# Group norms, key centring and scaled weights with PSUM operands or on ScalarE; joins that carry the ends of child stages

## The chip, the cores and the metric

The kernel runs on one core of one Trainium2 chip. The metric is the device time of one execution in microseconds, as a median of several runs. A profile is one more execution, taken by the hardware profiler. Its engines are PE (TensorE), PEld (TensorE's weight loads), DVE (VectorE), ACT (ScalarE), POOL (GpSimd) and SP (SyncE, which here only issues DMAs).

## The reference, cut to what matters

The input is x, eight images of 56 x 56 x 192 in float32. Two layers follow each other, each of them a group norm, a block and a residual.

```python
def _gn(v, G=32, eps=1e-5):          # 32 groups of 6 channels, over all positions
    g = v.reshape(B, H, W, G, C // G)
    m = mean(g, axis=(1, 2, 4)); s = var(g, axis=(1, 2, 4))
    return ((g - m) / sqrt(s + eps)).reshape(v.shape)

# layer 0: attention with convolved projections
q  = pointwise(batch_norm(depthwise3x3(_gn(x), stride 1)))   # 3136 tokens, 3 heads of 64
kv = pointwise(batch_norm(depthwise3x3(_gn(x), stride 2)))   # 784 keys
x  = x + softmax(q k^T * 64**-0.5) v @ out_w + out_b

# layer 1: a selective scan in four directions
xa, z = split(in_proj_w @ _gn(x))              # 384 channels each
xc = silu(depthwise3x3(xa) + conv_b)
for k in range(4):                             # row-wise, column-wise, and both reversed
    dts, Bs, Cs = split(x_proj_weight[k] @ xc)
    delta = softplus(dt_projs_weight[k] @ dts + dt_projs_bias[k])
    h = exp(delta * A) * h + delta * B * xc    # 16 states per channel, along 3136 positions
    y += sum_over_states(h * C) + D * xc
x = x + (layernorm(y) * silu(z)) @ out_proj_w.T
```

## The kernel before, in words

An image is worked in seven chunks of T = 448 positions (NCH = 7), with the channels on the partitions: 192 channels are two blocks (NB) of 96 (CP), 384 are three (NJ) of 128.

**The scan** is the long part. For each image there are four directions (in the order 0, 1, 3, 2), seven chunks and 16 states, thus 448 steps. A step takes these turns: `inputs_made` has POOL form du times the broadcast row of B into one of seven h buffers (L1175); `decays` has ACT form exp(delta * A) into a PSUM bank (L1189); `scans` has DVE run the recurrence, three instructions for the three blocks (L1206), and `carries` keeps its last column (L1228). Of 16 states, POOL scales and adds three by C itself (L1304, L1308); for the others PE transposes h (L1252, four bundles of three), ACT scales the result by C (L1268) and PE transposes back into the accumulator y (L1286). DVE adds y into yacc at a chunk's end (L1338, L1340). The rows of B and C come by DMA as broadcasts (`bb`, five buffers, and `cb`).

**The preparation** of the next image runs beside the scan of this one. `front` loads the image, transposes it and takes its statistics (`part`), forms the group norm's scale and shift (`group_norm`), normalizes (`normal`, ACT, L538), convolves and projects to q, k and v, centres the keys and bounds the scores (the loop over `kts`, L693 to L707), attends, takes the second group norm, scales the input weights by it (`scaled_weights`, L475), projects and convolves. `x_proj` then makes the scan's inputs; its last stores are `du<-v`. `finish` normalizes yacc, gates it and projects it out; it scales the z weights anew, as `wz2`, once per image.

**The group norm** (`group_norm`, L447 to L465) merges the chunks' statistics per channel on DVE (bn_aggr), averages mean and variance over each group of six channels by a matmul with the block matrix `group`, squares the distance of the channel's mean from the group's, averages that by a second matmul, and forms rstd by Ln and Exp on ACT.

**The keys**: for each of three heads, DVE sums the keys over their 784 positions (L693), divides (L694), subtracts the mean from `kT` (L696), takes the largest absolute value (L698) and multiplies it into the bounds of q (`km`, L700). PE adds over the partitions (L703), and DVE turns the sums into the shift of the exponents, `nsh` (L706, L707).

**The order of the work** is written by a list scheduler that runs when the program is built (`Sched`). A stage is a generator that yields requests: engine, estimated cost, the cells it reads and writes. A cell holds the estimated time of its last write and read; a DMA's write comes at its stated latency plus MARGIN, 3.0 us. The scheduler gives out the request with the earliest t - rank, where t is not before the stage's start nor the engine's estimated free time. The result is a fixed order of instructions on each engine, and each engine works through its own in that order; semaphores alone hold it up. `front` is paced by the scan's progress (`pace`): within 12 us of PE time of a wanted share. PE gets small filler matmuls (L1418) where the plan leaves it a gap.

A stage's `start` bounds all its requests, and a child inherits it. `join` waits until the children are done and lifts the parent's `start` to their `end`. A stage's own `end` grows with its own requests alone. `arounds` runs, for each image, the stages `front(b + 1)` and then `x_proj(b + 1)`, each by a join; both do most of their work in children of their own.

SBUF for the preparation comes from pools that are opened and closed in turn, so that a tile of one stage can lie where a tile of the stage before it lay; the instruction that first writes it waits for the last reader. The two `pad` tiles of `front`, whose border columns are set to zero by four memsets (L511), are the first tiles written in an image's preparation.

Of the kernel before, what the change touches and what calls it, by code (L numbers as in the profile page):

```python
# [8 lines left out]
F32 = mybir.dt.float32  # L9
AF = mybir.ActivationFunctionType  # L10
ALU = mybir.AluOpType
# [8 lines left out]
CP = 96  # L20
NB = C // CP
# [6 lines left out]
HEADS, DH = 3, 64  # L28
KW = HW // 2
KEYS = KW * KW  # L30
# [4 lines left out]
NJ = DIN // 128  # L35
# [19 lines left out]
PE, ACT, DVE, POOL, SP = range(5)  # L55
# [110 lines left out]
class Sched:  # L166
# [25 lines left out]
    def join(self, stages):  # L192

        me = self.now
        yield lambda: all(s.done for s in stages)
        me.start = max([me.start] + [s.end for s in stages])

    def keep_busy(self, t):

# [75 lines left out]
def kernel(  # L275
# [24 lines left out]
    nc = tc.nc  # L300
# [21 lines left out]
    group = fill("group", [CP, CP], 1.0 / 6.0)  # L322
# [31 lines left out]
    for nm, src in (("q", bn_q), ("kv", bn_kv)):  # L354
        p = load(f"bn{nm}", [CP, 4, NB], src.rearrange("v (b p) -> p v b", p=CP))
        s = const.tile([CP, NB], F32, name=f"bns{nm}")
# [66 lines left out]
    gnp = ctx.enter_context(tc.tile_pool(name="gn", bufs=2))  # L423
# [10 lines left out]
    def bank():  # L434
        return banks[0]

    def group_norm(st, cells, layer):

        mv = gnp.tile([CP, NB, 2], F32, name="mv")
        gm = gnp.tile([CP, NB, 2], F32, name="gm")  # L440
        mean = gnp.tile([CP, NB], F32, name=f"mean{layer}")
        dm = gnp.tile([CP, NB], F32, name="dm")
        rstd = gnp.tile([CP, NB], F32, name=f"rstd{layer}")
        k = [Cell() for _ in range(6)]
        yield DVE, 0.3, cells, [k[0]]
        for bl in range(NB):
            nc.vector.bn_aggr(mv[:, bl, :], st[:, bl])  # L447
        pg = yield bank()
        yield PE, 0.2, [k[0]], pg.c
        nc.tensor.matmul(pg.ap[:CP, 0:2 * NB], group, mv.rearrange("p b s -> p (b s)"), start=True, stop=True)  # L450
        yield DVE, 0.6, pg.c, [k[1]]
        nc.vector.tensor_copy(gm.rearrange("p b s -> p (b s)"), pg.ap[:CP, 0:2 * NB])
        pg.free()
        nc.vector.tensor_copy(mean, gm[:, :, 0])
        nc.vector.tensor_tensor(dm, mv[:, :, 0], mean, ALU.subtract)
        nc.vector.tensor_tensor(dm, dm, dm, ALU.mult)
        pd = yield bank()
        yield PE, 0.2, [k[1]], pd.c
        nc.tensor.matmul(pd.ap[:CP, 0:NB], group, dm, start=True, stop=True)
        yield DVE, 0.2, pd.c, [k[2]]  # L460
        nc.vector.tensor_tensor(rstd, pd.ap[:CP, 0:NB], gm[:, :, 1], ALU.add)
        pd.free()
        yield ACT, 0.5, [k[2]], [k[3]]
        nc.scalar.activation(rstd, rstd, AF.Ln, bias=eps[:CP])
        nc.scalar.activation(rstd, rstd, AF.Exp, scale=-0.5)  # L465
        return mean, rstd, k[3]

    def scaled_weights(w, cell, half, rstd, k):

        got = Cell()  # L470
        yield SP, 0.07, [], [got], 5.0
        nc.sync.dma_start(w, in_wT.rearrange("(b p) o -> p b o", p=CP)[:, :, half * DIN:(half + 1) * DIN])
        yield DVE, 0.6, [got, k], [cell]
        for bl in range(NB):
            nc.vector.tensor_scalar(w[:, bl], w[:, bl], rstd[:, bl:bl + 1], None, ALU.mult)  # L475

    def dma(reads, writes, late, dst, src, after=()):
        yield SP, 0.07, reads, writes, late
# [7 lines left out]
    def front(b):  # L486
# [12 lines left out]
        st = gnp.tile([CP, NB, NCH, 6], F32, name="st")  # L499
        with tc.tile_pool(name=f"fx_{b}", bufs=2) as pool:  # L500
            fx = Rings(pool, 2)
            k_st = [Cell() for _ in range(NCH)]
# [39 lines left out]
                               pad.ap, [pad])  # L542

            yield from sc.join([sc.spawn(part(c)) for c in range(NCH)])
            mean, rstd, k_rs = yield from group_norm(st, k_st, 0)
            off, k_gn = gnp.tile([CP, NB], F32, name="off"), Cell()
            yield DVE, 0.3, [k_rs], [k_gn]
            nc.vector.scalar_tensor_tensor(off, mean, -1.0, rstd, ALU.mult, ALU.mult)
            yield from sc.join([sc.spawn(normal(c)) for c in range(NCH)])

        with tc.tile_pool(name=f"kv_{b}", bufs=1) as kvp:
# [7 lines left out]
            k_qm = [[Cell() for _ in range(NCH)] for _ in range(2)]  # L559
# [8 lines left out]
            qms = [kvp.tile([128, NCH], F32, name=f"qm{i}") for i in range(2)]  # L568
# [117 lines left out]
            pn = yield bank()  # L686
            for h, kt in enumerate(kts):
                kk = [Cell() for _ in range(4)]
                ks = gnp.tile([128, 1], F32, name=f"ks{h}")
                kx = gnp.tile([128, 1], F32, name=f"kx{h}")  # L690
                km = kvp.tile([128, NCH], F32, name=f"km{h}")
                yield DVE, 1.1, k_k[h // 2] + [k_z], [kk[0]]
                nc.vector.tensor_reduce(ks, kt, AX.X, ALU.add)  # L693
                nc.vector.tensor_scalar(ks, ks, 1.0 / KEYS, None, ALU.mult)  # L694
                yield DVE, 0.6, [kk[0]], [kk[1]]
                nc.vector.tensor_scalar(kt, kt, ks, None, ALU.subtract)  # L696
                yield DVE, 0.9, [kk[1]], [kk[2]]
                nc.vector.tensor_reduce(kx, kt, AX.X, ALU.max, apply_absolute_value=True)  # L698
                yield DVE, 0.1, [kk[2]] + k_qm[h // 2], [kk[3]]
                nc.vector.tensor_scalar(km, qms[h // 2], kx, None, ALU.mult)  # L700
                k_km.append(kk[1])
                yield PE, 0.1, [kk[3]], pn.c if h == HEADS - 1 else []
                nc.tensor.matmul(pn.ap[:TP, h * NCH:(h + 1) * NCH], ones, km, start=True, stop=True)  # L703
            nv = nsh.rearrange("p h c -> p (h c)")
            yield DVE, 0.3, pn.c, [k_ns]
# [4 lines left out]
            st1 = gnp.tile([CP, NB, NCH, 6], F32, name="st1")  # L710
            k_st1 = [Cell() for _ in range(NCH)]
# [90 lines left out]
                yield from sc.join(ends)  # L802


        mean1, rstd1, k_gn1 = yield from group_norm(st1, k_st1, 1)
        nbias = gnp.tile([128, 2 * NJ], F32, name="nbias")
        k_nb = Cell()
        with tc.tile_pool(name=f"fw_{b}", bufs=1) as fw, tc.tile_pool(name=f"fi_{b}", bufs=2) as pool:
# [6 lines left out]
            pn = yield bank()  # L815
            for i, w in enumerate((wx, wz)):
                yield PE, 1.2, [k_w[i], k_gn1], pn.c if i else []
                for j in range(NJ):
                    for bl in range(NB):
                        nc.tensor.matmul(pn.ap[:, i * NJ + j:i * NJ + j + 1], w[:, bl, j * 128:(j + 1) * 128],  # L820
                                         mean1[:, bl:bl + 1], start=(bl == 0), stop=(bl == NB - 1))
            yield DVE, 0.1, pn.c, [k_nb]
            nc.vector.tensor_scalar(nbias, pn.ap[:, :2 * NJ], -1.0, None, ALU.mult)
            pn.free()
            made[b] = dict(
                x1d=x1d, xcs=xcs, k_x1=k_x1, k_xcs=k_xcs, rstd=rstd1, nbias=nbias, k_gn=k_gn1, k_nb=k_nb,
# [295 lines left out]
    chunks, brow, crow, das, states, news, ys = {}, {}, {}, {}, {}, {}, {}  # L1122
# [107 lines left out]

    def y_of(i):

        if i not in ys:
            t = yield ry
            free = Cell()
            free.w = t.c[0].r
            at["y"] = i
            ys[i] = dict(t=t, free=free, on=False, left=[(NST - len(by[i])) * SUB + sum(z for _, z in by[i].values())] * NJ)
        return ys[i]
# [105 lines left out]
    with tc.manual_schedule():  # L1345
# [11 lines left out]
        with ExitStack() as es:  # L1357
# [4 lines left out]
            ry = Ring(lambda: ybanks, 1)  # L1362
# [127 lines left out]
```

## Time and profile before

| | |
|---|---|
| median of 3 runs | 17656.52 us (17656.25 to 17665.69) |
| profiled execution | 17659.74 us, span 17658.0 us |
| granted TensorE clock, mean | 0.973 |
| PE, PEld, DVE, ACT, POOL busy | 15853.6, 11086.3, 14092.1, 14192.0, 15553.4 us |
| DMA moved, mean rate | 2373.32 MB, 134 GB/s |

The busy times are averages over stages with different limits, so they are read together with stretches of the span. A group of instructions is told by its line, engine, operation, output and inputs; the mean duration is that of one instruction and includes any time for which it is held up once it has been issued. Idle time before an instruction is put down to what ended it.

### The profile page before, as it was taken

The page shows a single profiled execution, that of the slowest core. Times are in us where ns is not written, and L with a number is a line of the kernel's source. Part 1 is how long each engine was busy: PE and PEld are TensorE (multiplying, and loading weights), DVE is VectorE, ACT ScalarE, POOL GpSimd, SP SyncE. Part 2 cuts the span into 40 slices and gives each one's busy share as a digit, 9 for nine tenths or more (in the row PEclk, how much of TensorE's full clock was granted, in tenths as well). Part 3 has the DMA queues.
Part 4 walks back from the last instruction along what each step waited for, and adds up shares of the span by engine and source line. Part 5 has one row for each costly group of instructions (what it writes and reads, how often), then busy time and mean ns, then how long its engine had stood idle before and what let it go on. Part 6 is the DMA issues. An engine that isn't in the chain of part 4 may idle for free. (4 is left out here: it accounts for less than half of the span.)

```text
span 17658.0 us, 282202 instructions
## 1 busy us (share of the span) xinstructions
PE 15853.6 (90%) x101550; PEld 11086.3 (63%) x101550; DVE 14092.1 (80%) x17871; ACT 14192.0 (80%) x25030; POOL 15553.4 (88%) x5200
## 2 busy tenths in 40 slices
PE   7699989998989989899898998989989898999998
PEld 4366666666666656666566666666656666667776
DVE  2378877888778878788787887878878888789898
ACT  3478887788877888788787887878888788889888
POOL 0489889898998989899898998989989899899998
PEclk9899999999999999999999999999999999999999
DMA  2653465435553365533645336453364434643332
GB/s 75 203 163 98 131 180 154 115 98 158 157 162 110 99 165 160 158 101 100 177 154 155 100 99 188 146 154 98 104 194 145 143 101 116 181 146 115 96 101 77
DMA packets 1508343, 2373.32 MB, mean 134 GB/s; under 512 B 197104, under 2 KB 1498912, under 8 KB 1503872
## 3 DMA queue, kind: packets, MB, share of 16 engines
q1 hardware_dynamic: 1506944, 2355.25, 45.8%
q8 instruction: 806, 13.21, 0.3%
q14 instruction: 593, 4.86, 0.1%
HBM read 1803.75 MB, written 550.97 MB: 133 GB/s over the span
## 5 line engine op out<-in xcount | busy, mean ns | idle before, releaser
L1206 DVE TENSOR_TENSOR_SCAN h<-da,newc,h 128x448 f32<-128x448 f32 x9216 | 10083.4, 1136 | 1717.6 <-ACT da L1189 1400.8
L1175 POOL TENSOR_TENSOR h<-du_s,bb 128x1344 f32<-128x1344 f32 x3584 | 10827.0, 3055 | 598.0 <-PE ht L1252 506.4
L1189 ACT ACTIVATE da<-dl_s,acoef 128x448 f32<-128x448 f32 x10752 | 6589.3, 636 | 839.2 <-DVE h L1206 420.2
L1268 ACT ACTIVATE g<-ht,ct_s 112x384 f32<-112x384 f32 x10864 | 5943.0, 578 | 1330.8 <-PE ht L1252 1123.0
L1252 PE MATMUL ht<-ident,h 128*112 128x128 f32 x32592 | 5209.4, 278 | 317.7 <-DVE h L1206 225.3
L1286 PE MATMUL y<-ident,g 112*128 112x112 f32 x32592 | 4909.1, 269 | 619.0 <-ACT g L1268 479.3
L1286 PEld LDWEIGHTS y<-ident,g 112*128 112x128 f32 x32592 | 3532.2, 142 | 2599.9 <-ACT g L1268 1663.8
L1252 PEld LDWEIGHTS ht<-ident,h 128*112 128x112 f32 x32592 | 3677.1, 135 | 1012.9 <-DVE h L1206 458.4
L1206 DVE TENSOR_TENSOR_SCAN h<-da,h 128x448 f32<-128x448 f32 x1536 | 1589.9, 1076 | 331.6 <-ACT da L1189 240.7
L1304 POOL TENSOR_TENSOR h<-h,cb 128x1344 f32<-128x1344 f32 x420 | 1282.0, 3052 | 476.4 <-DVE newc L1228 245.2
L1418 PE MATMUL y<-zeros 128*128 128x64 f32 x12318 | 1650.9, 272 | 0.0
L1418 PEld LDWEIGHTS y<-zeros 128*128 128x128 f32 x12318 | 1591.7, 197 | 56.7 <-issue 56.6
L1304 POOL TENSOR_TENSOR yp<-h,cb 128x1344 f32<-128x1344 f32 x448 | 1367.0, 3051 | 274.7 <-DVE h L1206 165.7
L1308 POOL TENSOR_TENSOR yp<-yp,h 128x1344 f32<-128x1344 f32 x420 | 1279.4, 3046 | 32.8
L1323 PE MATMUL y<-yp,ident 128*128 128x448 f32 x2688 | 1221.3, 552 | 7.4 <-POOL yp L1308 7.0
L976 POOL TENSOR_TENSOR v<-v,xs 128x1344 f32<-128x1344 f32 x224 | 678.6, 3050 | 591.3 <-DMA dl<-v 586.1
L782 PE MATMUL bank<-qT,kT 128*112 128x448 f32 x2352 | 1054.1, 566 | 141.0 <-DVE oT L745 90.1
L791 PE MATMUL bank<-pT,vt 112*128 112x448 f32 x2352 | 1019.1, 544 | 25.8 <-ACT pT L732 21.5
L732 ACT ACTIVATE pT<-bank,nsh 112x448 f32<-112x448 f32 x1176 | 743.6, 634 | 198.4 <-PE bank L782 159.5
L782 PEld LDWEIGHTS bank<-qT,kT 128*112 128x112 f32 x2352 | 360.6, 177 | 534.6 <-DVE oT L745 120.0
L1009 PE MATMUL bank<-xd,dtw 128*128 128x448 f32 x1344 | 632.9, 572 | 39.9 <-DVE h L1206 10.5
L1228 DVE TENSOR_REDUCE newc<-h 128x3 f32<-128x3 f32 x3584 | 563.2, 157 | 103.7
(146 smaller groups left out, 9950.6 us busy)
## 6 DMA issues: line engine op xcount, KB each, us to landing
bb<-rows SPq DMA_DIRECT2D x3584, 224.0 KB, 3.4
cb<-rows SPq DMA_DIRECT2D x868, 224.0 KB, 3.6
dl<-v SPq DMA_DIRECT2D x224, 672.0 KB, 5.1
du<-v SPq DMA_DIRECT2D x224, 672.0 KB, 5.2
du_s<-du SPq DMA_DIRECT2D x224, 672.0 KB, 4.5
dl_s<-dl SPq DMA_DIRECT2D x224, 672.0 KB, 4.5
stack<-xpd SPq DMA_DIRECT2D x504, 232.0 KB, 5.0
xt<-x1d SPq DMA_DIRECT2D x224, 336.0 KB, 5.7
```

Source lines behind the costliest of these rows:

```text
L782: nc.tensor.matmul(ps.ap[:TP, :T], kts[h][:, kb * TP:(kb + 1) * TP], qh.ap, start=True, stop=True)
L791: nc.tensor.matmul(po.ap[:, :T], vt[:, kb, g:g + 2, :].rearrange("p g d -> p (g d)"), pts[kb].ap, start=(kb == 0), stop=(kb == NKB - 1))
L1175: nc.gpsimd.tensor_tensor(h.ap, du.ap, bb.ap.unsqueeze(1).to_broadcast([128, NJ, T]), ALU.mult)
L1189: nc.scalar.activation(da.ap[:, :T], dl.ap[:, j], AF.Exp, scale=acoef[:, k * NJ + j, n:n + 1])
L1206: nc.vector.tensor_tensor_scan(h.ap[:, j, rev], da.ap[:, 0:T][:, rev], h.ap[:, j, rev], news[i - 1].ap[:, j, n:n + 1] if ci else 0.0, ALU. ...
L1252: nc.tensor.transpose(ht.ap[:TP, j * 128:(j + 1) * 128], h.ap[:, j, s * TP:(s + 1) * TP], ident)
L1268: nc.scalar.activation(g.ap, ht.ap[:TP, :DIN], AF.Copy, scale=ct.ap[:, s, n:n + 1])
L1286: nc.tensor.matmul(y["t"].ap[:, j, s * TP:(s + 1) * TP], g.ap[:, j * 128:(j + 1) * 128], ident[:TP, :TP], is_transpose=True, start=(n == 0 ...
L1304: nc.gpsimd.tensor_tensor(to.ap, h.ap, cbr.ap.unsqueeze(1).to_broadcast([128, NJ, T]), ALU.mult)
L1308: nc.gpsimd.tensor_tensor(yp.ap, yp.ap, h.ap, ALU.add)
L1323: nc.tensor.matmul(y["t"].ap[:, j, :T], ident, yp.ap[:, j], start=False, stop=(y["left"][j] == 0))
L1418: nc.tensor.matmul(ybanks[:, 0, T:T + FILL], zeros, zeros[:, :FILL], start=False, stop=False)
```

## The change

In `Sched.join` the parent's `end` is lifted to its new `start`, so that a stage whose work lies in children hands their end on to the stage that joins it.

`group_norm` copies the group's values out of PSUM no longer before it uses them. The differences take the group's mean from PSUM, one of the two factors of the square is itself written to PSUM (`apart`), the second matmul goes to other columns of the same bank, the mean is kept negated (`nmean`), and the shift `off` = -mean * rstd is made on ACT, for both layers.

`scaled_weights` multiplies on ACT instead of DVE. In the key loop, the subtraction of the mean and the multiplication by the largest absolute value go to ACT; the two reductions and the division stay on DVE. The costs given to the scheduler are changed with the instructions.

`nbias` is a copy, as the mean is negated already. `y_of` waits until the accumulator is either taken for this chunk or free.

```diff
@@ Sched.join
         me.start = max([me.start] + [s.end for s in stages])
+        me.end = max(me.end, me.start)
@@ group_norm
-        gm = gnp.tile([CP, NB, 2], F32, name="gm")
-        mean = gnp.tile([CP, NB], F32, name=f"mean{layer}")
         dm = gnp.tile([CP, NB], F32, name="dm")
+        within = gnp.tile([CP, NB], F32, name="within")
+        nmean = gnp.tile([CP, NB], F32, name=f"nmean{layer}")
         rstd = gnp.tile([CP, NB], F32, name=f"rstd{layer}")
+        off = gnp.tile([CP, NB], F32, name=f"off{layer}")
-        yield DVE, 0.3, cells, [k[0]]
+        yield DVE, 0.55, cells, [k[0]]
         for bl in range(NB):
             nc.vector.bn_aggr(mv[:, bl, :], st[:, bl])
         pg = yield bank()
-        yield PE, 0.2, [k[0]], pg.c
+        of_group = pg.ap[:CP, 0:2 * NB].rearrange("p (b s) -> p b s", s=2)
+        apart, spread = pg.ap[:CP, 8:8 + NB], pg.ap[:CP, 16:16 + NB]
+        yield PE, 0.3, [k[0]], pg.c
         nc.tensor.matmul(pg.ap[:CP, 0:2 * NB], group, mv.rearrange("p b s -> p (b s)"), start=True, stop=True)
-        yield DVE, 0.6, pg.c, [k[1]]
-        nc.vector.tensor_copy(gm.rearrange("p b s -> p (b s)"), pg.ap[:CP, 0:2 * NB])
+        yield DVE, 0.5, pg.c, [k[1]]
+        nc.vector.tensor_tensor(apart, mv[:, :, 0], of_group[:, :, 0], ALU.subtract)
+        nc.vector.tensor_tensor(dm, mv[:, :, 0], of_group[:, :, 0], ALU.subtract)
+        nc.vector.tensor_tensor(dm, dm, apart, ALU.mult)
+        nc.vector.tensor_scalar(nmean, of_group[:, :, 0], -1.0, None, ALU.mult)
+        nc.vector.tensor_copy(within, of_group[:, :, 1])
+        yield PE, 0.3, [k[1]], [k[2]]
+        nc.tensor.matmul(spread, group, dm, start=True, stop=True)
+        yield DVE, 0.2, pg.c + [k[2]], [k[3]]
+        nc.vector.tensor_tensor(rstd, spread, within, ALU.add)
         pg.free()
-        nc.vector.tensor_copy(mean, gm[:, :, 0])
-        nc.vector.tensor_tensor(dm, mv[:, :, 0], mean, ALU.subtract)
-        nc.vector.tensor_tensor(dm, dm, dm, ALU.mult)
-        pd = yield bank()
-        yield PE, 0.2, [k[1]], pd.c
-        nc.tensor.matmul(pd.ap[:CP, 0:NB], group, dm, start=True, stop=True)
-        yield DVE, 0.2, pd.c, [k[2]]
-        nc.vector.tensor_tensor(rstd, pd.ap[:CP, 0:NB], gm[:, :, 1], ALU.add)
-        pd.free()
-        yield ACT, 0.5, [k[2]], [k[3]]
+        yield ACT, 1.0, [k[3]], [k[4]]
         nc.scalar.activation(rstd, rstd, AF.Ln, bias=eps[:CP])
         nc.scalar.activation(rstd, rstd, AF.Exp, scale=-0.5)
-        return mean, rstd, k[3]
+        for bl in range(NB):
+            nc.scalar.activation(off[:, bl:bl + 1], nmean[:, bl:bl + 1], AF.Copy, scale=rstd[:, bl:bl + 1])
+        return nmean, rstd, off, k[4]
@@ scaled_weights
-        yield DVE, 0.6, [got, k], [cell]
+        yield ACT, 1.05, [got, k], [cell]
         for bl in range(NB):
-            nc.vector.tensor_scalar(w[:, bl], w[:, bl], rstd[:, bl:bl + 1], None, ALU.mult)
+            nc.scalar.activation(w[:, bl], w[:, bl], AF.Copy, scale=rstd[:, bl:bl + 1])
@@ front, after the statistics
-            mean, rstd, k_rs = yield from group_norm(st, k_st, 0)
-            off, k_gn = gnp.tile([CP, NB], F32, name="off"), Cell()
-            yield DVE, 0.3, [k_rs], [k_gn]
-            nc.vector.scalar_tensor_tensor(off, mean, -1.0, rstd, ALU.mult, ALU.mult)
+            _, rstd, off, k_gn = yield from group_norm(st, k_st, 0)
@@ front, the loop over kts
                 nc.vector.tensor_reduce(ks, kt, AX.X, ALU.add)
-                nc.vector.tensor_scalar(ks, ks, 1.0 / KEYS, None, ALU.mult)
-                yield DVE, 0.6, [kk[0]], [kk[1]]
-                nc.vector.tensor_scalar(kt, kt, ks, None, ALU.subtract)
+                nc.vector.tensor_scalar(ks, ks, -1.0 / KEYS, None, ALU.mult)
+                yield ACT, 0.9, [kk[0]], [kk[1]]
+                nc.scalar.activation(kt, kt, AF.Identity, bias=ks)
                 yield DVE, 0.9, [kk[1]], [kk[2]]
                 nc.vector.tensor_reduce(kx, kt, AX.X, ALU.max, apply_absolute_value=True)
-                yield DVE, 0.1, [kk[2]] + k_qm[h // 2], [kk[3]]
-                nc.vector.tensor_scalar(km, qms[h // 2], kx, None, ALU.mult)
+                yield ACT, 0.2, [kk[2]] + k_qm[h // 2], [kk[3]]
+                nc.scalar.activation(km, qms[h // 2], AF.Copy, scale=kx)
                 k_km.append(kk[1])
-                yield PE, 0.1, [kk[3]], pn.c if h == HEADS - 1 else []
+                yield PE, 0.2, [kk[3]], pn.c if h == HEADS - 1 else []
@@ front, the second norm
-        mean1, rstd1, k_gn1 = yield from group_norm(st1, k_st1, 1)
+        nmean1, rstd1, _, k_gn1 = yield from group_norm(st1, k_st1, 1)
...
-                                         mean1[:, bl:bl + 1], start=(bl == 0), stop=(bl == NB - 1))
+                                         nmean1[:, bl:bl + 1], start=(bl == 0), stop=(bl == NB - 1))
             yield DVE, 0.1, pn.c, [k_nb]
-            nc.vector.tensor_scalar(nbias, pn.ap[:, :2 * NJ], -1.0, None, ALU.mult)
+            nc.vector.tensor_copy(nbias, pn.ap[:, :2 * NJ])
@@ y_of
+        yield lambda: i in ys or ry.ready()
         if i not in ys:
             t = yield ry
```

## The prediction

> **What bounds the kernel now.** I read the page first. Its busy line is near balance and settles nothing:
>
> ```profile
> PE 15853.6 (90%) x101550; PEld 11086.3 (63%) x101550; DVE 14092.1 (80%) x17871; ACT 14192.0 (80%) x25030; POOL 15553.4 (88%) x5200
> ```
>
> So I cut the span by stage. The scan runs from 695 us to the end, in eight images; images two to seven take about 2150 us each and repeat the same pattern, the last, with no preparation beside it, 1752. The fifth image (9393 to 11550) stands for the others. Columns: busy time of PE, weight loads, DVE, ACT, POOL, then granted clock.
>
> ```profile
> core 0: us, PE busy (x) PEld busy (x) DVE busy (x) ACT busy (x) POOL busy (x), PEclk, DMA share, GB/s
> 9477.50:9492.60 15.10, 4.95 (x43) 4.43 (x41) 0.05 (x3) 1.98 (x4) 2.53 (x1) 0.77 0.87 324
> 9554.40:9560.20 5.80, 0.85 (x8) 0.74 (x6) 5.11 (x4) 0.00 (x0) 5.72 (x3) 0.75 0.37 112
> 9560.20:9570.20 10.00, 10.00 (x49) 10.00 (x49) 5.69 (x7) 6.52 (x12) 2.31 (x1) 0.50 0.51 91
> 9783.70:9802.70 19.00, 14.22 (x71) 11.34 (x70) 18.09 (x19) 3.10 (x7) 18.02 (x6) 0.73 0.55 137
> 9802.70:9816.00 13.30, 13.30 (x59) 10.03 (x59) 7.04 (x9) 8.48 (x15) 0.02 (x1) 0.74 0.07 20
> 11036.40:11042.70 6.30, 5.08 (x27) 3.21 (x27) 6.30 (x4) 6.27 (x8) 6.22 (x3) 1.00 0.51 167
> 9900.00:10300.00 400.00, 372.64 (x2201) 251.33 (x2201) 345.53 (x428) 359.93 (x669) 391.48 (x131) 1.00 0.35 101
> ```
>
> The last row is the undisturbed scan: POOL works 98% of it, so GpSimd's products are the pace there. The other rows are holes. In the first everything stops; in the second DVE runs four tiny instructions for 5 us while ACT does nothing, and in the third POOL pays, working 2.31 us of 10. PE's full rows are filler matmuls, at half clock. I therefore price a stall by the POOL gap behind it, since POOL's lost time is what the undisturbed rate cannot give back. DVE's groups show what the tiny instructions are (mean ns after the busy time):
>
> ```profile
> L475 DVE TENSOR_SCALAR wz<-wz,rstd 96x384 f32<-96x384 f32 x32 | 78.6, 2495 | 0.2 <-DMA wz<-in_in_wT_dram 0.2
> L696 DVE TENSOR_SCALAR kT<-kT,ks 128x784 f32<-128x784 f32 x24 | 44.5, 1855 | 0.9
> L700 DVE TENSOR_SCALAR km<-qm,kx 128x7 f32<-128x7 f32 x24 | 39.1, 1629 | 0.8
> L454 DVE COPY mean<-gm 96x2 f32<-96x2 f32 x16 | 33.9, 2120 | 0.6
> L455 DVE TENSOR_TENSOR dm<-mv,mean 96x2 f32<-96x2 f32 x16 | 30.2, 1888 | 0.5
> L461 DVE TENSOR_TENSOR rstd<-bank,gm 96x2 f32<-96x2 f32 x16 | 2.5, 156 | 9.2 <-PE bank L459 9.2
> ```
>
> L455 and L461 have the same shape and operation. L461, with a PSUM operand, takes 155 to 157 ns in all 16 cases; L455, on SBUF alone, 156 to 2929. The short cases lie in the start-up, where POOL runs nothing beside them. The timeline gives what follows each hole (brackets: idle time, and who ended it):
>
> ```profile
> 9492.56 0.14 DVE L511 MEMSET pad<- 96x16 f32 x3 [15.05 <-issue]
> 9494.00 3.02 POOL L1304 TENSOR_TENSOR h<-h,cb 128x1344 f32<-128x1344 f32 x1 [13.97 <-DVE newc L1228]
> 9570.34 3.05 POOL L1175 TENSOR_TENSOR h<-du_s,bb 128x1344 f32<-128x1344 f32 x1 [7.83 <-PE ht L1252]
> 9802.50 0.64 ACT L1189 ACTIVATE da<-dl_s,acoef 128x448 f32<-128x448 f32 x1 [15.50 <-DVE nsh L706]
> 9815.98 3.04 POOL L1175 TENSOR_TENSOR h<-du_s,bb 128x1344 f32<-128x1344 f32 x1 [14.18 <-PE ht L1252]
> ```
>
> **What the Trainium skill says.** "SBUF — State Buffer", section "Who interferes with whom": VectorE and GpSimd share one pair of SBUF ports under an exclusive lock held for a whole instruction. A copy or tensor_scalar in a two-port mode needs it, and so does a DVE instruction with two SBUF inputs against a GpSimd instruction that reads SBUF; a tensor_reduce never does. The trace agrees: waits reach about one POOL product (3.05 us), and the reduce at L698 takes 969 to 973 ns always. "VectorE: DVE Perf Modes", section "Why PSUM operands drop a tier", says a PSUM operand excludes the two-port mode; L461 agrees. "TensorE: Matmul & The Clock Gate", Part 1, says that an idle array falls to half clock; the 0.50 row agrees.
>
> **The change, part by part.** Every SBUF-alone instruction it names waited. Against the start-up durations (L475 0.41, L696 0.63, L700 0.23, the rest 0.16 us), the excess over the run is 219 us: per image about 5.5 in the first group norm, 9.1 in the key stage, 5.8 in the second norm, 4.9 in the weights behind it and 5.5 in the weights of finish. The memset at L511 waited another 85 us (4.3, 10.0, then 14 on average in five images). DVE loses 266 us of busy time (L475, L454 to L456, L548, L696, L700) and L452's 2.5, and gains five PSUM operations of 0.16 us in each of 16 norms, 12.6 us. No row shows DVE writing PSUM, as `apart` is; I take L461's 0.16, and at twice that the 16 would cost 2.5 us more.
>
> *First group norm.* POOL gaps 7.83 and 3.29, 11.1 us. The chain from bn_aggr to off took 8.3 us, of it lock 5.5. Two thirds of the gap goes: 7.3 x 7 = 51 us. The rest stays, because two PE round trips and ACT's Ln and Exp remain.
>
> *Key stage.* DVE held for 19.0 us, POOL's gap 14.2. After the change DVE keeps three times 0.95 + 0.15 + 0.97 and 0.36, 6.6 us, broken up by ACT's turns so that scans fit between. I leave 2 us of gap. The clamp at L707 is still SBUF alone; it ran at 178 ns because POOL was then stopped, and may now wait up to 3 us. I take 1.5. Gain 10.7 x 7 = 75 us. ACT's 15.5 us wait at nsh goes, because the planner charged this stage 8.1 us and the new costs, 9.3, are near what the rows add up to.
>
> *Second norm and its weights.* POOL gaps 4.2, 2.6, 1.1 and 3.3, 11.3 us; lock 10.7 of a DVE time of 17. Two thirds: 7.5 x 7 = 53 us.
>
> *Weights in finish.* 5.5 us of lock, but POOL has no gap in or after it (6.22 of 6.30, and 12.30 of the next 12.30). The filled h buffers hide it: 1 us x 7, and 2 in the last image, 9 us. Without that cover it would be worth 5.5 x 7 + 4 = 43.
>
> *The join.* front's start now carries the modelled end of x_proj, 4.5 + 3.0 us behind the last du store. So the four memsets and the first xin loads are ordered later, and SP is no longer parked between 9482.8 and 9492.3 with bb rows behind it. The stores in that window took about 10 us from issue, with DMA at 0.87, so I leave 3 us per image. POOL's share is 13.97 of 15.05, so 85 becomes 79, less 21: 58 us. x_proj's xpw and dtw loads also move behind front's last store; their POOL-side effect has no row. PE waited about 2 us for xs there, so I bound it at 2 us per image either way and take 0.
>
> *ACT's new work.* From L1062 (659 ns, SBUF, one pointer operand, 448 columns) and 0.83 ns per element ("ScalarE: Activation LUTs", section "What ACT_TABLE_LOAD costs"; the trace has 665 ns for 896 columns, 0.74, between L1062 and L1073), I estimate 0.61 for a weight half, 0.94 for kT and 0.295 for the tiny ones (L464's duration). That is 48 x 0.61 + 24 x 0.94 + 24 x 0.295 + 32 x 0.295 = 68 us, 60 beside scans. Nine instructions per image also wait on ACT for DVE or a load, with da and g queued behind them, and scans and transposes waiting for those. The usual wait of ACT for a small DVE result is 0.8 us (padded, 49.5 over 63), so 9 x 7 x 0.8 = 50. POOL-bound stretches hide most; I charge a quarter of 110, 28 us. Ends: 0 and 110. The new test in y_of issues nothing: 0.
>
> Sum: 51 + 75 + 53 + 9 + 58 - 28 = 218 us off. The profiled execution took 17659.7 us (span 17658.0), so 17441.7; it lies 3.2 above the median of 17656.5, so I predict **17440 us**, with 17330 to 17540 as this case's own range.
>
> **The rivals.** *Absorbed:* the scan catches up, and only the join and ACT's nsh wait pay, about 80 us: 17575. For it: at the finish weights POOL never stopped. Against it: POOL's gaps behind the other four. *Knock-on:* the static order was laid out for times that the holes broke. POOL idles 191 us per image, only 50 of which I touch; if the truer order recovers as much again of what follows the holes, 400 us go: 17255. *Slower:* ACT becomes the place of the wait. It feeds both the scans (1641 us of DVE waits) and the turns back (1664 us of weight loads). If each of the nine new ACT waits holds it for 5.5 us with nothing hidden, 7 x 9 x 5.5 = 347 and 60 of work beat the 246 gained: 17815. It decides from (246 - 60) / 63 = 3.0 us per wait. For it: ACT waited 9 us per norm at L464. Against it: that wait was the lock itself. *It does not do what it says:* a new order meets other collisions and gives the gain back: 17650.
>
> **How the numbers follow.** Forecast 0.54, absorbed 0.16, knock-on 0.15, slower 0.10, nothing 0.05. A measurement of this kernel tells about 0.2%, 35 us, from no change. Faster takes the first three, 0.85; same 0.05; slower 0.10. The range 17190 to 17610 leaves out the slower and the null case and the far end of the knock-on, below two in ten with the ends of ACT's price (0 to 110) inside.
>
> **What would show it.** Right: the norm and key operations on DVE at 0.16 and 0.95 us, ACT's wait at Ln under 3 us a time instead of 9, no 15 us hole at the memset, POOL idle near 150 us per image. Wrong: ACT gaps before the weight scaling or the kT activation above 3 us, L707 at 3 us, or the same POOL gaps with other names in front of them.

## The result, and the profile after

The changed kernel takes **17394.4 us** (median of 4 runs, 17388.0 to 17406.6), against 17661.1 of the kernel before on the same chip: a ratio of **0.9845, 95% interval 0.9831 to 0.9859**, some 267 us off. The forecast was 17440, 46 us too high. Its profiled span is 17404.9 us, at a granted clock of 0.982.

The busy line of the page after:

```profile
PE 15710.1 (90%) x101140; PEld 10967.3 (63%) x101140; DVE 13834.0 (79%) x17783; ACT 14251.9 (82%) x25158; POOL 15546.4 (89%) x5200
```

DVE lost 258 us of busy time, ACT gained 60 and POOL, the pace of the scan, is where it was. So the 267 us are not work that POOL was spared. They are idle time of POOL: 183 to 196 us per image before (images two to seven), 139 to 158 after. To see where, here are the stretches of the fifth image that answer to those shown of before, from the table of windows of the changed kernel (columns as before: PE, weight loads, DVE, ACT, POOL, granted clock):

```profile
core 0: us, PE busy (x) PEld busy (x) DVE busy (x) ACT busy (x) POOL busy (x), PEclk, DMA share, GB/s
9341.20:9348.00 6.80, 3.74 (x26) 2.52 (x25) 0.17 (x1) 2.03 (x4) 6.80 (x3) 1.00 1.05 395
9398.90:9404.10 5.20, 4.65 (x42) 4.13 (x41) 3.76 (x12) 3.46 (x10) 5.20 (x2) 1.00 0.54 189
9404.10:9414.10 10.00, 9.15 (x79) 8.26 (x78) 7.90 (x10) 8.86 (x16) 8.64 (x4) 1.00 0.76 185
9630.20:9642.20 12.00, 11.33 (x82) 8.55 (x81) 11.82 (x18) 11.18 (x22) 11.92 (x5) 1.00 0.32 66
9642.20:9655.50 13.30, 12.18 (x55) 6.80 (x54) 8.25 (x11) 10.24 (x19) 13.30 (x5) 1.00 0.62 178
9755.00:10155.00 400.00, 368.88 (x2198) 250.91 (x2197) 338.78 (x415) 359.18 (x667) 388.50 (x130) 1.00 0.35 98
```

The rows are the memset hole, the first norm, the 10 us behind it, the key stage, what follows that, and the undisturbed scan. The hole is 6.8 us long where it was 15.1, and POOL works right through it. In the norm DVE issues 12 instructions in 5.2 us, among them scans, where it issued four in 5.8. The 10 us behind it have 8.64 us of POOL instead of 2.31. The key stage takes 12.0 us instead of 19.0, and the 13.3 us after it, in which POOL did nothing before, are now full. The granted clock is 1.00 in all of them; before, it was 0.50 to 0.77 in the first five. In the undisturbed scan POOL works 97% of the time, where it was 98%.

The groups of DVE and then of ACT (busy time, mean ns of one, idle time before), after the memset's group of the kernel before:

```profile
L511 DVE MEMSET pad<- 96x16 f32 x32 | 1.3, 72 | 85.1 <-DMA du<-v 51.6 <-issue 29.3 <-POOL yp L1308 4.3
```

```profile
L456 DVE TENSOR_TENSOR bank<-mv,bank 96x2 f32<-96x2 f32 x16 | 2.5, 157 | 8.7 <-PE bank L454 8.7
L458 DVE TENSOR_TENSOR dm<-dm,bank 96x2 f32<-96x2 f32 x16 | 2.4, 153 | 0.6
L464 DVE TENSOR_TENSOR rstd<-bank,within 96x2 f32<-96x2 f32 x16 | 2.4, 152 | 4.4 <-PE bank L462 4.4
L709 DVE TENSOR_SCALAR nsh<-nsh 112x21 f32<-112x21 f32 x8 | 7.2, 905 | 0.3
L516 DVE MEMSET pad<- 96x16 f32 x32 | 1.3, 72 | 35.3 <-DMA dl_s<-dl 14.0 <-DMA du<-v 7.4 <-issue 7.0
```

```profile
L698 ACT ACTIVATE kT<-kT,ks 128x784 f32<-128x784 f32 x24 | 22.8, 949 | 11.6 <-DVE ks L696 11.6
L480 ACT ACTIVATE wz<-wz,rstd 96x384 f32<-96x384 f32 x32 | 17.8, 604 | 0.0
L702 ACT ACTIVATE km<-qm,kx 128x7 f32<-128x7 f32 x24 | 7.2, 300 | 5.3 <-DVE kx L700 3.6
L467 ACT ACTIVATE rstd<-rstd,eps 96x2 f32<-96x2 f32 x16 | 4.7, 296 | 82.1 <-DVE rstd L464 82.1
```

No DVE instruction of the norm waits any more. L456, which writes its result into PSUM, takes 157 ns, hardly more than L458 and L464, which only read it. The clamp, L709, is the only instruction on DVE whose duration still varies by more than 0.2 us, so the only one that still waits for the port: 0.9 us where it took 0.18. It can be read as the price of a POOL that no longer stands still beside it. The division of the key sums (L696, 128x1, SBUF alone) and the reductions did not wait before and do not now. On ACT the new operations take what was estimated (0.95, 0.60, 0.30 us) and wait 0.5 us at kT and 0.2 at km. Its wait at Ln is 82.1 us, 44.4 of it once in the start-up; the other 15 come to 2.5 us each, against 6.7 before. The memsets still wait 35 us in all, of 85.

In the key stage DVE and ACT take turns, and scans fit in between. From the timeline of DVE in the changed kernel:

```profile
9630.64 0.94 DVE L695 TENSOR_REDUCE ks<-kT 128x1 f32<-128x784 f32 x1
9631.62 0.15 DVE L696 TENSOR_SCALAR ks<-ks 128x1 f32<-128x1 f32 x1
9631.69 1.14 DVE L1208 TENSOR_TENSOR_SCAN h<-da,newc,h 128x448 f32<-128x448 f32 x1
9632.85 0.97 DVE L700 TENSOR_REDUCE kx<-kT 128x1 f32<-128x784 f32 x1
```

What is late next is the convolution of `front`. In the timeline of POOL, the gap at it was 10.8 and 9.1 us before; after, it is

```profile
9471.44 3.05 POOL L1307 TENSOR_TENSOR h<-h,cb 128x1344 f32<-128x1344 f32 x1 [20.36 <-issue]
9493.20 3.06 POOL L1307 TENSOR_TENSOR yp<-h,cb 128x1344 f32<-128x1344 f32 x1 [9.59 <-DVE newc L1230]
```

In the 20.3 us before the first of these PE is busy for 19.5 us, nearly all of it with the matmuls of the convolution and the projections behind it, and few of the scan's transposes come between. The profile names nothing that ended this gap ("issue"), so that PE holds the scan up here is likely and not shown. The two gaps together grew from 19.9 to 30.0 us in this image, and by 5 to 10 us in each of images three to seven: part of what was gained before them is lost here again.

### The profile page after: what moved, and what is told of

Read it like the earlier page. It is cut to its first block, busy times and chain, and to the rows that moved or that the text cites. A ratio compares the mean times of both kernels' runs of the same rounds, so it can differ in the third digit from the quotient of the medians.

```text
span 17404.9 us, 281492 instructions
## 1 busy us (share of the span) xinstructions
PE 15710.1 (90%) x101140; PEld 10967.3 (63%) x101140; DVE 13834.0 (79%) x17783; ACT 14251.9 (82%) x25158; POOL 15546.4 (89%) x5200
## 5 line engine op out<-in xcount | busy, mean ns | idle before, releaser
L1421 PE MATMUL y<-zeros 128*128 128x64 f32 x11908 | 1561.1, 268 | 0.0
L1421 PEld LDWEIGHTS y<-zeros 128*128 128x128 f32 x11908 | 1501.1, 193 | 53.1 <-issue 53.1
L1011 PE MATMUL bank<-xd,dtw 128*128 128x448 f32 x1344 | 631.8, 572 | 33.9 <-DVE v L1014 11.2
```

Of the source, the lines that this page charges most:

```text
L1421: nc.tensor.matmul(ybanks[:, 0, T:T + FILL], zeros, zeros[:, :FILL], start=False, stop=False)
```

## The experiments

Theory: the small instructions held DVE, and POOL behind it, for as long as the shared SBUF port was POOL's; taking them off the port gives back about two thirds of that time, part by part. Rivals: the order that the new costs lay out does it; the stalls are hidden or move elsewhere. A ratio is to runs of the kernel before that were taken beside it on the same chip, with a 95% interval, for most kernels some 25 us to each side. A gain in us is the difference of the two medians. (Some expectations take gains from the ratios, which compare means, and so have 67, 72 and 16 us where 69, 69 and 18 stand here.) The planner is the scheduler. Comparisons by stage are taken in the traces, between the ends of the last scan instruction of each chunk; a quarter of an image is one direction, seven chunks, and "per image" is the mean of images three to seven. The excess of an instruction is its time above what it takes where POOL is idle.

**One part alone.** Four kernels take one part of the change each into the kernel before. First the join, with the test in `y_of`:

```diff
         me.start = max([me.start] + [s.end for s in stages])
+        me.end = max(me.end, me.start)
```

> The join and the test in y_of alone, all small operations as before. Theory (each part pays its own POOL gap): only the hole at the pad memsets shrinks, its idle time on DVE from 85 us to about 35, POOL's idle time in images three to seven falls by about 8 us each, and the time falls by 58 us to about 17600 (17570 to 17630). Rival (the order matters as a whole: the two halves need each other): the join alone re-lays the front against wrong costs of the locked operations and gives nothing or a loss, 17640 to 17700, and the sum of the single parts falls short of the whole 262 us by more than 100.

Measured: 17590.8 us, ratio 0.9962 (0.9947 to 0.9977), 69 us off. The memset wait fell from 85 to 33 us. The first two chunks, where the hole is, gained 7.3 us per image; another 9.1 came from the last three chunks of the third quarter and the first of the fourth, where `front` ends and `x_proj` begins.

Then the group norm, its diff as shown for the change:

> The group norm alone (PSUM operands, off on ACT, the negated mean, with its planner costs) and the test in y_of; join, keys and weights as before. Theory: the lock of 5.5 and 5.8 us per image goes in the two norms, L464's wait on ACT falls from 144 us to under 90, and the time falls by about 51 + 29 = 80 us to 17580 (17540 to 17620). Rival (what follows the first norm, the convolutions, is paced by the front and takes the time back, as the trace of the whole change suggests, where chunks 1 and 2 of direction 0 gained nothing): only the second norm pays, 20 to 40 us, about 17630.

Measured: 17728.2 us, ratio **1.0041** (1.0026 to 1.0056), 69 us **slower**; neither expected that. The norm's own instructions ran free of the lock. But the next one of that chain did not. The group of the weight scaling before and in this kernel, and the timelines of DVE and of POOL around one case here (a count above 1 is that many instructions in a row):

```profile
L475 DVE TENSOR_SCALAR wx<-wx,rstd 96x384 f32<-96x384 f32 x16 | 10.3, 684 | 4.1 <-DMA wx<-in_in_wT_dram 4.1
L479 DVE TENSOR_SCALAR wx<-wx,rstd 96x384 f32<-96x384 f32 x16 | 94.7, 5958 | 4.0 <-DMA wx<-in_in_wT_dram 4.0
```

```profile
8476.00 13.46 DVE L479 TENSOR_SCALAR wx<-wx,rstd 96x384 f32<-96x384 f32 x2
8489.38 0.14 DVE L1229 TENSOR_REDUCE newc<-h 128x3 f32<-128x3 f32 x1
```

```profile
8464.97 12.04 POOL L1176 TENSOR_TENSOR h<-du_s,bb 128x1344 f32<-128x1344 f32 x4
8476.98 3.02 POOL L1306 TENSOR_TENSOR yp<-h,cb 128x1344 f32<-128x1344 f32 x1
8479.97 8.94 POOL L1176 TENSOR_TENSOR h<-du_s,bb 128x1344 f32<-128x1344 f32 x3
8489.66 3.03 POOL L1176 TENSOR_TENSOR h<-du_s,bb 128x1344 f32<-128x1344 f32 x1 [0.75 <-DVE newc L1229]
```

A wx half took 0.41 us in the median before, 3.2 at most. Now the first of an image's two waits 13 us, once in each of seven images, through five POOL products that follow each other without a pause, and gets the port when POOL has run out of inputs, because it waits for DVE itself. Before, `mean` and `dm` had spent that time a few steps earlier. **The wait had moved.** That is not the whole loss. In the fourth quarter 8.4 us per image went in no instruction that waits for the port. And image two alone, which the means leave out, lost 35 us, half of the 69; 29 of them went in its third and fourth chunk, again without such a wait. There POOL stands still once for 48 us, for a transpose on PE, where its longest gap was 21. From the timelines of POOL, before and here:

```profile
3168.52 3.07 POOL L1304 TENSOR_TENSOR h<-h,cb 128x1344 f32<-128x1344 f32 x1 [20.52 <-issue]
```

```profile
3212.77 6.18 POOL L1176 TENSOR_TENSOR h<-du_s,bb 128x1344 f32<-128x1344 f32 x2 [47.93 <-PE ht L1254]
```

So the order that the norm's requests gave has a large share in the loss, beside the moved wait.

The key loop alone:

> The key loop alone (subtraction and product on ACT, with its costs). Theory: DVE's run of 19.0 us becomes about 11 with ACT's turns, the lock of 9.1 us per image goes and ACT's wait at nsh (93 us) with it; 10.7 us per image, 75 us in all, 17585 (17550 to 17610). If the whole change's chunk 4 (13.6 us per image shorter) is all the keys' own, it is 95 us, 17565. Rival (the absorbed case): POOL is the pace and only the ACT wait pays, under 40 us, 17620 to 17650.

Measured: 17641.3 us, ratio 0.9991 (0.9982 to 1.0000), 18 us off instead of 75. The key chunk itself gained 14.4 us per image, more than the 10.7 expected; but the second quarter gave back 9 and the third 7, while the wait of `mean` (L454) grew from 33.9 to 72.6 us and the clamp's from nothing to 9.

The scaled weights alone on ACT:

```diff
-        yield DVE, 0.6, [got, k], [cell]
+        yield ACT, 1.05, [got, k], [cell]
...
-            nc.vector.tensor_scalar(w[:, bl], w[:, bl], rstd[:, bl:bl + 1], None, ALU.mult)
+            nc.scalar.activation(w[:, bl], w[:, bl], AF.Copy, scale=rstd[:, bl:bl + 1])
```

> The three weight scalings alone on ACT. Theory: the second-norm pair pays two thirds of its lock of 4.9 us, 3.4 per image, finish 1 per image: about 33 us less 10 of ACT's time, 17635 (17610 to 17660). Rival (DVE time is worth its length wherever it is lost, no cover by the filled h buffers): 4.9 + 5.5 us per image, about 75 us, 17585. Rival (ACT is the wrong place, its waits cost more than the lock): slower, 17680 or more.

Measured: 17598.4 us, ratio 0.9966 (0.9953 to 0.9979), 61 us off; the rival's full length (75) is nearer than the theory's 23. Of the three parts that free instructions it is the only one whose lock time went without turning up elsewhere: all such excess over the run fell from 219 to 147 us, against 179 with the norm freed, which alone had 85, and 187 with the keys freed, which had 63.

The four sum to -69 + 69 - 18 - 61 = -79 us; the whole change gives -267. **The parts are not additive.**

**What the lock costs, by itself.** One instruction on 96 x 2 elements is added to the changed kernel at each of the 224 chunk ends, once with two SBUF inputs and once with a PSUM one:

```diff
             nc.vector.tensor_tensor(yv, pv, yv, ALU.add)
+            nc.vector.tensor_tensor(probe, zeros[:CP, 0:2], probe, ALU.mult)   # or: y.ap[:CP, 0, 0:2]
```

> The whole change plus one tensor_tensor of 96x2 on DVE behind each of the 224 evictions of y, both inputs in SBUF, not told to the planner, so the order stays. Compared with the twin whose first input is in PSUM. Theory: it waits for POOL's product as L455 did, 1.2 to 1.9 us on average, 270 to 430 us in all, and two thirds of that shows in the span: 180 to 280 us above the twin. Rival (absorbed; DVE's time at a chunk's end is covered by the filled h buffers): under 80 us above the twin. Rival (the memory of the operand is not what matters): equal to the twin.

> The twin: the same 224 instructions with the first input in PSUM (y itself), the second in SBUF. Theory: 0.16 us each, 36 us of DVE time, at most 30 us above the whole change, 17395 to 17425, none of them longer than 0.2 us. Rival (any DVE instruction in this place costs, whatever it reads): the same loss as the SBUF one.

Measured: 18195.9 us with SBUF operands (ratio 1.0311, 1.0284 to 1.0338) and 17414.0 with the PSUM one (0.9859, 0.9844 to 0.9874). The two groups, one of each kernel:

```profile
L1345 DVE TENSOR_TENSOR probe<-zeros,probe 96x2 f32<-96x2 f32 x224 | 830.9, 3709 | 0.0
```

```profile
L1345 DVE TENSOR_TENSOR probe<-y,probe 96x2 f32<-96x2 f32 x224 | 32.7, 146 | 0.0
```

An instruction of 0.15 us costs 3.7 us on average. The busy time differs by 798 us and the run time by 782: at this place nearly every microsecond of the lock reached the end, not two thirds. Single cases took 143 ns to 13.4 us. One of 11.5 us, in the timelines of DVE and of POOL of the SBUF kernel:

```profile
2541.96 11.53 DVE L1345 TENSOR_TENSOR probe<-zeros,probe 96x2 f32<-96x2 f32 x1
2553.42 2.18 DVE L1209 TENSOR_TENSOR_SCAN h<-da,newc,h 128x448 f32<-128x448 f32 x2
```

```profile
2538.47 9.06 POOL L1178 TENSOR_TENSOR h<-du_s,bb 128x1344 f32<-128x1344 f32 x3
2547.45 6.03 POOL L979 TENSOR_TENSOR v<-v,xs 128x1344 f32<-128x1344 f32 x2
2556.78 3.03 POOL L1308 TENSOR_TENSOR yp<-h,cb 128x1344 f32<-128x1344 f32 x1 [3.30 <-DVE h L1209]
```

The wait runs past the ends of three POOL instructions and is over at the fourth, with which POOL's supply ends; then POOL itself waits 3.3 us for the scan that DVE could not run. "SBUF — State Buffer", section "Who interferes with whom", has the lock held for a whole instruction. The trace agrees, but it shows more: between two POOL instructions that follow without a pause, a waiting DVE instruction mostly does not get in. At 240 such ends a probe was waiting; it was passed over at 153 of them and got in at 87. Another 116 of the 224 probes got in where POOL paused, and 21 did not wait. So it is not semaphores alone that hold an engine up in its order; the port does so too.

**The lock without the order.** All these instructions are freed inside the old requests, with their old costs and without the join, so that the planner lays out the order of before:

```diff
+        nc.vector.tensor_tensor(apart, mv[:, :, 0], of_group[:, :, 0], ALU.subtract)
+        nc.vector.tensor_tensor(dm, mv[:, :, 0], of_group[:, :, 0], ALU.subtract)
+        nc.vector.tensor_tensor(dm, dm, apart, ALU.mult)
...
-                nc.vector.tensor_scalar(kt, kt, ks, None, ALU.subtract)
+                nc.scalar.activation(kt, kt, AF.Identity, bias=ks)
```

> All three small-operation parts in the order of before: the requests and costs given to the planner are those of before, only the instructions behind them differ (norm operands in PSUM with one difference written there; off, kT, km and the weights on ACT). No join. Theory A (the lock is worth its POOL gaps in any order): about 188 us for norms, keys and weights less 28 of ACT's time, 160 us, 17500 (17450 to 17550). Theory B (what the single parts lost, norm alone 72 us slower and keys alone only 16 faster, is the price of a re-laid order, not of the operations): at least as fast as A, 17430 to 17520, with direction 1 at 472 us and not 480. Rival C (the stretch around each hole catches up, so removing locks does little by itself): 17580 to 17640.

Measured: 17502.6 us, ratio 0.9908 (0.9892 to 0.9925), **159 us off**, as theory A had it: three quarters of the 214 us of lock time that went (219 before, 5 left, all at the clamp). Per image the first norm's chunk gained 5.4 us, the keys' 8.1, that of the second norm and its weights 10.4; the second quarter did not move.

**The join inside the change**, once by leaving it out of the changed kernel, once by adding it to the last one:

```diff
-        me.end = max(me.end, me.start)
```

> The whole change without the one line in join. If the parts add, the join is worth here what it is worth alone, 69 us: 17460 (17430 to 17490), with the hole at the pad memsets back at 85 us in all. Rival (join and costs need each other): 17520 or more, near the sum of the parts without the join, which is no gain at all, 17655. Rival (the rest already hides it): under 30 us, below 17425.

> The kernel before with every lock-taking instruction freed inside the old requests and costs (as in the run that took 17502.6), and now the join that carries the ends of child stages, with its test in y_of. So it differs from the changed kernel only in the requests and costs that the planner sees in the norm, the keys and the weights. Theory A (the join is worth what it is worth in the changed kernel, 124 us, because stages without locks can use the order it gives; the new costs are worth next to nothing): 17661 - 159 - 124 = 17378, say 17370 to 17405, the changed kernel's own time. Theory B (the join is worth what it is worth alone, 67 us, and the rest of the change is the planner's truer costs): 17435, so 40 us slower than the changed kernel. Theory C (the old costs spoil the order once the join has moved the loads): above 17470.

Measured: without it 17518.5 us (ratio 0.9920, 0.9905 to 0.9935), 143 us off, so it is worth 124 us in the changed kernel; added to the old order it gives 17388.0 (0.9851, 0.9837 to 0.9866), 261 us off, so it is worth 102 us there. (The plain medians lie 115 us apart, but on two chips, on which the kernel before differed by 13.) The test in `y_of` was not run alone: it stays in both kernels of the first pair and comes with the join in the second. Theory A held: that kernel, with the old requests and costs, is as fast as the changed one, 261 us off and 267. The truer costs are worth nothing that shows. They move time about (keys another 4 us per image and the second norm 7 better, the second quarter 6 and the first norm's chunks 4 worse).

**Does the wait migrate?** The norm and the weights together, in the kernel before:

> The kernel before with the group norm's and the scaled weights' parts of the change together (and the test in y_of, which issues nothing), keys and join as before. The norm alone was 69 us slower, the weights alone 61 us faster. Theory M (migration: with the norm alone, the lock wait moved to the next instruction of the same chain, the weight scaling of the second norm, 13 us once per image; with both freed there is nothing left in that chain to take it): far below the sum of the single parts, 17540 to 17580, about 100 us off, since with all three freed in the old order the same stretches gave 5.4 + 10.4 us in each of seven images. Rival R (the norm's slowness lay in the order that its changed requests gave, and the parts add up): 17661 + 69 - 61 = 17669, within 20. In between, at 17600 to 17640, both had a share. The weight scaling is then ACT's at 0.61 us; the wait on the keys and the mean in the key stage should not fall.

Measured: 17568.9 us, ratio 0.9951 (0.9936 to 0.9966), 80 us off, where the single parts sum to +8. Migration holds: with the weights on ACT too, the second norm's chunk is 11.9 us per image faster, where the norm alone had made it 4.4 slower. The fourth quarter keeps its 9 us loss, and image two its loss of 28 us in two chunks, so these belong to the order that the norm's new requests lay out. In the whole change the first is gone and the second is 6 us; without the join the first is back, at 8.3 us per image.

**Only the costs.** The kernel before with all its locks, but with the planner told what they take:

```diff
-        yield DVE, 0.6, pg.c, [k[1]]
+        yield DVE, 6.0, pg.c, [k[1]]
...
-        yield DVE, 0.6, [got, k], [cell]
+        yield DVE, 5.0, [got, k], [cell]
```

> The kernel before with all its locks; only the costs told to the planner for the five lock-taking requests are raised to what they take with the lock (norm 0.6 to 6.0, off 0.3 to 1.2, weight halves 0.6 to 5.0, key subtraction 0.6 to 2.3, km 0.1 to 1.9 us), and the test in y_of. No instruction is removed or moved to another engine. Theory P (what hurts is the order laid out for wrong times: given the true times, the planner fits scans around the holes): 17550 to 17600. Theory L (it is the lock itself: an instruction on DVE's queue still stops DVE, and POOL behind it, wherever it stands): 17640 to 17680. A loss of over 50 us is possible too if the later order brings new waits; then the order alone moves the time by as much as a part of the change does.

Measured: 17671.8 us, ratio 1.0012 (1.0005 to 1.0019), 23 us slower. An order that knows of the waits does not avoid them: the excess is 228 us, where it was 219. Theory L. Two of the groups:

```profile
L454 DVE COPY mean<-gm 96x2 f32<-96x2 f32 x16 | 40.2, 2515 | 0.6
L696 DVE TENSOR_SCALAR kT<-kT,ks 128x784 f32<-128x784 f32 x24 | 49.6, 2068 | 0.9
```

**One step further.** The changed kernel with the clamp, the last instruction of the preparation that waits for the port, taken off it, and a later time for du's store:

```diff
-            nc.vector.tensor_scalar(nv, pn.ap[:TP, :HEADS * NCH], -SCALE, CAP, ALU.mult, ALU.add)
-            nc.vector.tensor_scalar(nv, nv, 0.0, None, ALU.min)
+            nc.vector.tensor_scalar(pn.ap[:TP, :HEADS * NCH], pn.ap[:TP, :HEADS * NCH], -SCALE, CAP, ALU.mult, ALU.add)
+            nc.vector.tensor_scalar(nv, pn.ap[:TP, :HEADS * NCH], 0.0, None, ALU.min)
...
-                    yield from dma([k_du[i]], [m["k_du"][lay + 2 * i, c]] + v.c[i * NJ:i * NJ + NJ], 4.5,
+                    yield from dma([k_du[i]], [m["k_du"][lay + 2 * i, c]] + v.c[i * NJ:i * NJ + NJ], 8.0,
```

> The changed kernel with two more edits of the same kind: the clamp of the key shifts works in PSUM (first tensor_scalar PSUM to PSUM, second PSUM to SBUF), so no instruction of the preparation takes the lock; and the planner is told that the du store lands 8.0 us after issue instead of 4.5, for the 35 us that DVE still waits at the pad memsets (about 14 of it behind du's stores). Theory 1 (lock and late store still cost what they show): clamp 6 us off, memset wait from 35 to 15 us, POOL's share of it 0.9: 17394 - 6 - 18 = 17370. Theory 2 (order decides: the later du shifts the first quarter of each image as any re-laid order did, by up to 10 us per image either way): 17330 to 17460, with the memset wait gone all the same.

Measured: 17361.1 us (17352.7 to 17364.9), ratio 0.9835 (0.9819 to 0.9852), the fastest of all. Its memset wait, from the groups of DVE:

```profile
L516 DVE MEMSET pad<- 96x16 f32 x32 | 1.3, 72 | 17.4 <-DMA du<-v 6.3 <-DMA cb<-rows 3.9 <-issue 3.7
```

It was 35.3 us, and no instruction of the preparation waits for the port now. Theory 1 (17370) is right to 9 us, but the range of theory 2 takes the time in as well, and its sign is there: against the changed kernel the first two chunks are 6.5 us shorter per image and the next two 8.2 longer. So what the memset gave did not stay, and which edit made the kernel faster, if either did, is open: the two were not run apart. Against the changed kernel's ratio the intervals overlap; against the kernel of 17388.0 us, which ran beside it on the same chip, the medians lie 27 us apart.

## Why the prediction was right

**The lock.** The prediction's four lock terms and ACT's price come to 51 + 75 + 53 + 9 - 28 = 160 us; freeing the lock in the old order gave 159. That small instructions hold DVE at the port, and POOL behind it, is right; that the sum is right to 1 us is luck, with an interval of some 30 us and terms that err both ways. To price a stall by POOL's gap behind it held in the sum, and so did its ingredients: DVE lost 258 us where 256 was worked out (266 + 2.5 - 12.6), ACT gained 60 where 68 was. The split is less good. First norm 5.4 us per image for 7.3, keys 8.1 for 10.7, second norm with weights 10.4 for 7.5. The weights of finish were put at 1 us because POOL did not stop there, and gave nothing measurable.

**The join.** This is the term that was mis-sized: 58 us predicted, 69 alone, 102 to 124 beside the freed locks. With an interval of some 25 us to each side of every ratio, that it is worth more there than alone is likely and not certain. The hole itself was about right (85 to 35 us of wait, where 21 was left). Added to the freed locks it gives 10.2 us per image in the first two chunks, the hole's place. But 7.6 more come at the end of the third quarter and the start of the fourth, where `front` ends and `x_proj` begins: "their POOL-side effect has no row" and "take 0" is the step that failed. It fails in the join alone too, with 9.1 us there and 7.3 at the hole; so the 69 lie near the 58 in part by luck. In the changed kernel it gives 8.4 at the hole, 2.5 there, and takes away the loss of the fourth quarter. What exactly is better placed stays open. The waits of PE for xs, which the prediction named, are not it: 95.9 us over the run became 88.9.

**Independent parts.** The sum treats the five parts as separate, and each lock wait as one that goes when its instruction goes, of "about one POOL product (3.05 us)". Both are wrong. A wait can last through five products, and with one instruction freed the next on the port can wait in its stead. The trace of before already had waits longer than one product: L454 once took 12.3 us, and L696 up to 5.1. The predicted gains would have been wrong for most parts taken alone: norm -80 expected, +69 measured; keys -75, -18; weights -23, -61. They came out in the sum, and the two kernels with more than one part freed fit the reason: the change takes off the port every waiting instruction but the clamp, so little was left for the wait to move to.

**The rivals.** *Slower* needed 3.0 us of ACT wait per turn; the turns at kT and km cost 0.5 and 0.2. *Knock-on* put a further gain on the truer order; costs alone gave +23 us, and the old costs with the join are as fast as the new ones. *Absorbed* falls with the 159 us. The null case, a new order that meets other waits and gives the gain back, did occur in the norm alone and, for the most part, in the keys alone, not in the whole.

**The marks.** Norm operations near 0.15 us, kT at 0.95, Ln's wait at 2.5 us, no 15 us hole, POOL's idle near 150 us per image: all seen. The clamp was given 1.5 us and took 0.9. Two readings of before were off without harm to the sum. ACT's "9 us per norm" at Ln counts 43.4 us of start-up; the other 15 waits were 6.7 each. And L461, a tensor_tensor, shows that a PSUM operand frees an instruction with two inputs; for the two-port modes of copies the case is L452, a copy from PSUM, at 157 to 159 ns in all 16.

## What to carry to other kernels

Where GpSimd works without a pause, a small VectorE instruction on SBUF alone is priced by GpSimd's queue, not by its size: here 3.7 us for 0.15. Not every one is: here the reductions and a tensor_scalar of one column never waited, so look at the spread of a group's durations first. Take off the port every waiting instruction of a chain, not the costliest one, since the next one can inherit the wait; give it a PSUM operand or put it on ScalarE. Before adding up the parts of such a change, ask which instruction would wait if only this one went, and test the parts both alone and left out, and once in the old order of instructions, which tells the operations from the order that their costs give.

## What the runs showed of the hardware

Two things had not been expected. A VectorE instruction that waits for the shared port is often passed over at the ends of GpSimd instructions that follow each other without a pause, at 153 of 240 such ends here: a wait of up to 13.4 us for 96 x 2 elements, with a mean of 3.7 us over 224 cases. And a VectorE operation that writes its result to PSUM from one SBUF and one PSUM input (L456, 157 ns) is no slower than one that writes to SBUF (L464, 152), so a scratch column in an open bank is a cheap way off the port.
